# One-hot rows on ScalarE for every batch, neighbour rows gathered in groups of four tiles, and a new order of work in a four-layer graph network

## The chip, the core and the metric

The kernel runs on one core of one Trainium2 chip. Five engines take part, each with its own queue of instructions that it works off in order: TensorE (PE in the profile, with its weight loads as PEld), VectorE (DVE), ScalarE (ACT), GpSimd (POOL) and SyncE (SP), which here only issues DMAs. ScalarE and GpSimd issue DMAs too. The metric is the device time in microseconds of one execution, as the median over several executions.

## What is computed

Input are 32 graphs ("batches") of 512 nodes with 128 features each, `x`, and a 0/1 adjacency matrix per graph, `adj`, in which about 3% of the entries are 1. Four layers follow each other, each with a layer norm and a ReLU ahead of it and a residual sum behind it. The first is a maximum over neighbours, the others are products with the adjacency matrix and with weights:

```python
# layer 0: edge maximum
p = einsum('bnd,do->bno', h, W1 - W2)
q = einsum('bnd,do->bno', h, W2)
x = x + max over j of relu(p[:, :, None, :] + q[:, None, :, :] + b) * adj[..., None]
# layer 1: four rounds, with features of earlier rounds appended
src_agg = einsum('bjv,bij->biv', src, l2norm(adj, 2))
dst_agg = einsum('bjv,bji->biv', dst, l2norm(adj, 1))
f = tanh(concat([src_agg, self_rep, dst_agg]) @ wu + bu)
# layer 2: mean over neighbours, then a weight
x = x + einsum('bnm,bmf->bnf', adj / rowsum, h @ weight) + bias
# layer 3: four GRU rounds
m = einsum('bjn,bjd->bnd', adj, hidden @ weight[i])
hidden = gru_cell(m, hidden, ...)
```

## The kernel before, in words

A batch's 512 nodes are four tiles (`NT = 4`) of 128 partitions. The kernel has no loop on the chip: all 32 batches are written out in one stream. Each batch goes through `prepare` (layer norm, transposed adjacency `at`, the products `qn` and `pn`, counts and keys of neighbours), `gathers` (the edge maximum), `layer1` and `layer23`.

The edge maximum needs, for every node, the largest row of `qn` among its neighbours. It is taken in two ways whose results are merged.

- By one-hot rows. For each of the four source tiles `jt` and each slot `k` of 1 to 4 (`KSLOT`), a 128x1024 one-hot matrix `oh` is made from counts `ccd`; two matmuls with the parts `qhl` pick the rows into a PSUM bank `pa`, and VectorE keeps the running maximum in `acc`. VectorE makes `oh` with one comparison (L1139), or ScalarE makes it with two activations, `far` and then `oh` (L1136 and L1137). How many of the four slots go to ScalarE is set by `ONACT` (L34), read by `min(b, len(ONACT) - 1)`: two for batches 0 and 1, one for batch 2, none from batch 3 on.
- By DMA. What lies beyond the slots is fetched row by row from a table `qtab` in device memory, by indices `idx`, seven rounds (`NLEFT`) for each of the four tiles, so 28 indirect DMAs a batch from GpSimd's queue. Round 0 lands in `gm`; every later row lands in a buffer `G` of one tile, of which there are four, and VectorE takes the maximum of `gm` and `G` for that tile (L1127).

`gm` and `acc` are merged in the stage "first". `parts` splits a feature matrix into `hi` (ScalarE) and `lo` (VectorE), or `sbuf_parts` makes `lo` on GpSimd; `aggregate` multiplies both with the adjacency into the bank `pg`. `pu` is the sum of a round of layer 1, `pk`, `phn` and `pxn` are the gates of layer 3. `gate`, `zc`, `nn`, `h` are the tensors of the GRU cell.

The order of instructions is not the order of the code. `Flow` records each operation with a cost and with what it depends on, and `step` then picks operations one by one as a planner: among those that could start first on an engine, the one with the earliest due time. A due time is `n * pace - due - lead` (L451): the place of the batch times `PACE`, less the planned work behind the operation, less a lead of its stage. Leads are in `LEADS`, with additions for the first and last batch in `LEADS0` and `LEADSN`; `FIRST`, `LAST` and `WEIGHTS` shift the places of the first batches, the last batches and the weight preparation. `SPACING` keeps the gathers' due times apart (`spaced`). Six parts are open at a time (`AHEAD`). Operations marked `port` are planned one at a time, since GpSimd and VectorE are taken to share an access to SBUF (L298). Where the planner sees TensorE idle for over a microsecond, it puts in filler matmuls, `spin` (L553), [...]whose result is not used.

All operations recorded this way carry line L529 in the profile, so the groups are read by the names of their tiles.

Of the kernel before, what the change touches and what calls it, by code (L numbers as in the profile page):

```python
# [13 lines left out]
F32 = mybir.dt.float32  # L14
# [10 lines left out]
P = 128  # L25
# [5 lines left out]
ROWS = 1024  # L31
KEY = float(ROWS)
CODES = ((0, 1), (P, 1), (2 * P, 2), (4 * P, 4))
ONACT = (2, 2, 1, 0)  # L34
NLEFT = 7
PACE = 46.14
SPACING = 1.5
AHEAD = 6
BANKS = (1, 2, 2, 1)

LEADS = {
    "prepare": -28.3, "counts": -7.5, "keys": 16.5, "rows": 26.6,
    "gather0": 59.4, "gather1": 70.0, "gather2": 28.0, "gather3": 53.5,
    "first": 61.2, "layer1": 43.0, "layer10": 30.3, "layer11": 8.7,
    "layer12": 56.0, "layer13": -41.3, "layer2": 39.7, "layer3": 5.5,
    "layer30": 99.5, "layer31": 189.8, "layer32": 213.5, "layer33": 84.7,
    "out": 56.0,
}

LEADS0 = {  # L50
    "prepare": 18.5, "counts": 53.1, "keys": 4.8, "rows": -15.7,
    "gather0": 52.2, "gather1": 93.4, "gather2": -34.5, "gather3": -69.1,
    "first": 0.5, "layer1": 141.7, "layer10": 10.1, "layer11": 110.3,
    "layer12": -73.8, "layer13": -13.4, "layer2": 6.9, "layer3": 56.5,
    "layer30": 35.3, "layer31": 29.8, "layer32": 117.9, "layer33": 64.0,
    "out": 75.9,
}
LEADSN = {
    "prepare": -19.9, "counts": -18.3, "keys": -42.0, "rows": 46.6,
    "gather0": 15.9, "gather1": -47.7, "gather2": -77.8, "gather3": -4.3,  # L60
    "first": 13.3, "layer1": -33.7, "layer10": 14.0, "layer11": -36.5,
    "layer12": 103.7, "layer13": 62.6, "layer2": 212.2, "layer3": 99.8,
    "layer30": 182.6, "layer31": 105.8, "layer32": 85.0, "layer33": 161.6,
    "out": -15.2,
}
FIRST = (1.57, 0.36, -0.05, 0.0)
LAST = (0.0, 0.18, 0.33, 0.24, 0.3)
WEIGHTS = (-3.98, -2.44, -5.94)

LATE = {  # L70
    "xn2": ("xn0", 1), "hi2": ("qn", 1), "lo2": ("gm", 1), "mT": ("acc", 1), "hg": ("hT0", 1),
# [114 lines left out]
def in_sbuf(v):  # L186
    return not isinstance(v, View) or v.tile.sbuf
# [86 lines left out]
class Engine:  # L274
# [5 lines left out]
    def __getattr__(self, op):  # L280
        fn = getattr(self.real, op)

        def note(*args, **kw):
            outs, ins = [], []
            for i, v in enumerate(args):
                (outs if i == 0 else ins).append(v)
            for k, v in kw.items():
                (outs if k in ("out", "accum_out") else ins).append(v)
            ins = [v.ap if isinstance(v, Rows) else v for v in ins]
            outs, ins = ([v for v in vs if hasattr(v, "free_size")] for vs in (outs, ins))  # L290
            cost, after = self.flow.cost(self.name, op, outs, ins)
            self.flow.note(self.name, fn, args, kw, outs, ins, cost, after)


            tensors = [v for v in ins if v.free_size() >= 64 and in_sbuf(v)]
            fast = self.name == "vec" and op == "tensor_scalar"
            if self.name == "vec" or (self.name == "pool" and op.startswith("tensor")):
                self.flow.part[-1].port = fast or len(tensors) > 1  # L298

        return note  # L300


class Flow:
# [46 lines left out]
    def fixed(self, t, shape, dtype):  # L350

        return View(Buf(None, 0, shape[0], t), shape, dtype)
# [270 lines left out]
class FastWeights:  # L623
# [5 lines left out]
    def __init__(self, nc, F, a, const, mid, ps):  # L629
        self.F, self.mid, self.ps = F, mid, ps  # L630
        self.NL3 = a["L3_gnn_weight"].shape[0]
        n = a["x"].shape[1]

        def fixed(shape, dtype, name):
            return const.tile(shape, dtype, name=name)

        ident = fixed([P, P], F32, "ident")
        make_identity(nc, ident)
        identb = fixed([P, P], BF16, "identb")
        nc.vector.tensor_copy(identb, ident)  # L640
        self.ident, self.identb = ident, identb
        self.mhalf = fixed([P, 8], F32, "mhalf")
        nc.gpsimd.memset(self.mhalf, -0.5)

        self.ones = fixed([P, P], F32, "ones")
        nc.gpsimd.memset(self.ones, 1.0)
        ltf = fixed([P, P], F32, "ltf")  # L650
        nc.gpsimd.affine_select(
            ltf, self.ones, pattern=[[1, P]], compare_op=ALU.is_ge, fill=0.0, base=0,
            channel_multiplier=-1,
        )
        nc.gpsimd.memset(ltf[0:HP, HP:P], 0.0)
        self.lt = fixed([P, P], F32R, "lt")
        nc.vector.scalar_tensor_tensor(self.lt, ident, NBASE, ltf, ALU.mult, ALU.add)
        self.ltk = fixed([P, P], BF16, "ltk")
        nc.vector.tensor_scalar(self.ltk, self.lt.bitcast(F32), KEY, None, ALU.mult)
        self.code = fixed([P, n // P, P], BF16, "code")  # L660
        icode, code = fixed([P, n // P], I32, "icode"), fixed([P, n // P], F32, "fcode")
        for t, (first, step) in enumerate(CODES):
            nc.gpsimd.iota(
                icode[:, t : t + 1], pattern=[[1, 1]], base=first, channel_multiplier=step
            )
        nc.vector.tensor_copy(code, icode)
        for t in range(n // P):
            nc.vector.tensor_scalar(
                self.code[:, t, :], ident, code[:, t : t + 1], None, ALU.mult
            )  # L670


        self.sign = fixed([P, 2], F32, "sign")
        nc.gpsimd.memset(self.sign[:, 0:1], -1.0)
        nc.gpsimd.memset(self.sign[:, 1:2], 1.0)
        nc.gpsimd.memset(self.sign[0:4, 0:1], 1.0)
        nc.gpsimd.memset(self.sign[0:4, 1:2], 0.0)

        self.slot = fixed([P, KSLOT + 1], F32, "slot")
        for k in range(KSLOT + 1):  # L680
            nc.gpsimd.memset(self.slot[:, k : k + 1], -(NBASE + k))
        self.nc, self.a, self.const, self.n = nc, a, const, n
        self.rows = self.zeros([P, n // P, P], "rows")
        self.vectors = []
        for i in range(2):
            t = fixed([P, P], F32, f"vectors{i}")
            nc.gpsimd.memset(t, 0.0)
            self.vectors.append(F.fixed(t, [P, P], F32))

    def own(self, shape, dtype, name):  # L690
        return self.F.tile(self.const, shape, dtype, name, name)
# [167 lines left out]
def fast(ctx: ExitStack, tc: tile.TileContext, a: dict, out: bass.AP, bad):  # L859
    nc = tc.nc  # L860
# [3 lines left out]
    NT = N // P  # L864

    const = ctx.enter_context(tc.tile_pool(name="const", bufs=1))
# [3 lines left out]

    F = Flow(nc, PACE, AHEAD)
    F.share(ps, 8, {f"ps{s}": n for s, n in enumerate(BANKS)} | {"idle": 0})
# [11 lines left out]
    big = ctx.enter_context(tc.tile_pool(name="big", bufs=1))  # L884
    mid = ctx.enter_context(tc.tile_pool(name="mid", bufs=1))
    W = FastWeights(nc, F, a, const, mid, ps)

    zero = const.tile([P, P], F32, name="zero")  # L890
    nc.gpsimd.memset(zero, 0.0)
    tables, scals = [], []
    for i in range(2):
        t = dram.tile([ROWS, P], F32, name=f"qtab{i}")
        k = (ROWS - 2 * P) // P
        nc.sync.dma_start(
            out=t[2 * P :, :].rearrange("(k p) d -> p k d", p=P),
            in_=zero.unsqueeze(1).to_broadcast([P, k, P]),
        )
        tables.append(F.fixed(t, [ROWS, P], F32))  # L900
        scals.append(F.fixed(dram.tile([6, N], F32, name=f"scal{i}"), [6, N], F32))
# [211 lines left out]
    def gathers(b, at, ccd, qhl, pn, tab, idx, has, dinv):  # L1113
        acc = F.tile(mid, [P, N], F32, tag="acc", name=f"acc_{b}")
        gm = F.tile(mid, [P, NT, P], F32, tag="gm", name=f"gm_{b}")
        for r in range(NLEFT):
            for it in range(NT):


                G = gm[:, it, :]  # L1120
                if r:
                    G = F.tile(big, [P, P], F32, tag="G", name=f"G_{b}_{it}_{r}", bufs=4)
                F.pool.indirect_dma_start(
                    out=G, out_offset=None, in_=tab, in_offset=Rows(idx[:, it, r : r + 1])
                )
                if r:
                    F.vec.tensor_max(gm[:, it, :], gm[:, it, :], G)  # L1127
                    F.spaced("gather", SPACING if b else 1.3)
        for jt in range(NT):
            F.lead = lead(b, f"gather{jt}")  # L1130
            for k in range(1, KSLOT + 1):
                oh = F.tile(big, [P, 2, N], F32R, tag="oh", name=f"oh_{b}_{jt}_{k}", bufs=3)
                if k > KSLOT - ONACT[min(b, len(ONACT) - 1)]:

# [224 lines left out]
    def spin(n):  # L1359
# [5 lines left out]
    places = [  # L1365
        b - FIRST[min(b, len(FIRST) - 1)] - LAST[max(0, b - B + len(LAST) - 1)] for b in range(B)
    ]
    F.run(
        list(zip(WEIGHTS, (W.first, W.rest, W.last)))
        + [(p, partial(batch, b)) for b, p in enumerate(places)]  # L1370
# [471 lines left out]
```

## Time and profile before

| what | us |
|---|---|
| median of three executions | 2909.99 (2907.28 to 2910.49) |
| the profiled execution | 2910.69 |
| its span, first to last instruction | 2909.0 |

The granted TensorE clock was 0.993 of full speed on average. Some groups that the text comes back to:

| group | engine | count | mean ns | busy us |
|---|---|---|---|---|
| oh<-ccd, 128x1024 | VectorE | 492 | 723 | 348.9 |
| gm<-gm,G, 128x128 | VectorE | 768 | 322 | 242.4 |
| acc<-acc,pa, 128x512 | VectorE | 992 | 679 | 673.4 |
| far<-ccd, 128x1024 | ScalarE | 20 | 1150 | 23.0 |
| oh<-far, 128x1024 | ScalarE | 20 | 1150 | 23.0 |
| G<-qtab, one tile's rows | GpSimd | 768 | 1095 | 841.3 |
| gate<-h,gate, 128x512 | GpSimd | 132 | 1326 | 175.1 |
| spin | TensorE | 233 | 400 | 64.1 |

A group is a set of instructions with the same tiles. "Out<-in" names the tile that is written and those that are read. Busy times of one engine can overlap at the edges of two instructions. Idle time of an engine is given with the instruction that ended it ("<- DVE lo" is a wait for VectorE's writing of `lo`). The chain of waits follows the last instruction back, at each step to what released it.

### The profile page before, as it was taken

The page shows a single profiled execution, that of the slowest core. Times are in us where ns is not written, and L with a number is a line of the kernel's source. Part 1 is how long each engine was busy: PE and PEld are TensorE (multiplying, and loading weights), DVE is VectorE, ACT ScalarE, POOL GpSimd, SP SyncE. Part 2 cuts the span into 40 slices and gives each one's busy share as a digit, 9 for nine tenths or more (in the row PEclk, how much of TensorE's full clock was granted, in tenths as well). Part 3 has the DMA queues.
Part 4 walks back from the last instruction along what each step waited for, and adds up shares of the span by engine and source line. Part 5 has one row for each costly group of instructions (what it writes and reads, how often), then busy time and mean ns, then how long its engine had stood idle before and what let it go on. Part 6 is the DMA issues. An engine that isn't in the chain of part 4 may idle for free.

```text
span 2909.0 us, 38588 instructions
## 1 busy us (share of the span) xinstructions
PE 2795.8 (96%) x11766; PEld 1794.6 (62%) x11766; DVE 2299.1 (79%) x5371; ACT 1268.4 (44%) x2622; POOL 1848.5 (64%) x2020
## 2 busy tenths in 40 slices
PE   7799999999999999999999999999999999999998
PEld 4565566666666665666665666666666666566675
DVE  6778888788888888888788888888888888887634
ACT  6643344444444443444443444444444444443333
POOL 3666656666666766666766666776666666666522
PEclk9999999999999999999999999999999999999999
DMA  6644334323444433334423344433344433333200
GB/s 150 136 74 88 62 85 81 83 55 76 79 86 81 83 60 78 74 83 80 87 56 78 74 84 87 82 69 64 74 84 87 81 81 56 70 66 63 55 5 9
DMA packets 191270, 218.49 MB, mean 75 GB/s; under 512 B 30376, under 2 KB 139600, under 8 KB 191056
## 3 DMA queue, kind: packets, MB, share of 16 engines
q0 software_dynamic: 47104, 92.34, 23.1%
q1 hardware_dynamic: 73768, 63.63, 7.1%
q10 hardware_dynamic: 70184, 59.98, 6.8%
q8 instruction: 96, 1.57, 0.2%
q14 instruction: 118, 0.97, 0.1%
HBM read 164.32 MB, written 17.96 MB: 63 GB/s over the span
## 4 chain that ended last, share of the span: by engine, by line
PE 85%; DVE 7%; DMA 2%; issue 2%; ACT 2%; POOL 1%; SPq 0%; ACTq 0%; DVEq 0%; POOLq 0%
PE pg L529 26%; PE pu L529 19%; PE pk L529 14%; PE pa L529 7%; PE phn L529 4%; PE pxn L529 4%; DVE acc L529 3%; PE ph L529 2%; PE pq L529 2%; PE pkey L529 2%; PE pt L529 1%; DVE lo L529 1%; PE pf L529 1%; PE po L529 1%; PE px L529 1%
## 5 line engine op out<-in xcount | busy, mean ns | idle before, releaser
L529 POOL DMA_INDIRECT G<-qtab,idx x768 | 841.3, 1095 | 653.6 <-DVE gm L529 495.3
L529 DVE TENSOR_TENSOR acc<-acc,pa 128x512 f32<-128x512 f32 x992 | 673.4, 679 | 123.3 <-PE pa L529 97.6
L529 PE MATMUL pg<-an,lo 128*128 128x512 f32 (+1 forms) x1072 | 461.9, 433 | 0.0
L529 PE MATMUL pg<-an,hi 128*128 128x512 f32 (+1 forms) x1072 | 456.1, 428 | 4.8 <-PE spin L553 1.1
L529 PE MATMUL pa<-oh,qhl 128*128 128x512 f32 x1024 | 450.5, 508 | 6.1 <-DVE acc L529 2.1
L529 PE MATMUL pu<-ag,w 128*128 128x512 f32 (+1 forms) x952 | 448.0, 568 | 4.1 <-DVE ag L529 4.1
L529 DVE TENSOR_SCALAR oh<-ccd 128x1024 fp32r<-128x1024 bf16 x492 | 348.9, 723 | 62.4 <-PE pa L529 55.0
L529 ACT ACTIVATE xn<-x,shift,rstd 128x128 f32<-128x128 f32 x512 | 214.6, 483 | 261.4 <-POOL shift L529 255.7
L529 PE MATMUL pg<-at,lo 128*128 128x512 f32 (+1 forms) x672 | 295.9, 442 | 22.8 <-DVE lo L529 22.3
L529 PE MATMUL pg<-at,hi 128*128 128x512 f32 (+1 forms) x672 | 272.7, 407 | 8.4 <-ACT hi L529 7.2
L529 PEld LDWEIGHTS pa<-oh,qhl 128*128 128x128 f32 x1024 | 191.8, 193 | 135.5 <-issue 65.9
L529 PEld LDWEIGHTS pg<-an,hi 128*128 128x128 f32 x1072 | 202.6, 189 | 107.2 <-issue 62.5
L529 PEld LDWEIGHTS pg<-an,lo 128*128 128x128 f32 x1072 | 202.7, 189 | 85.9 <-issue 52.0
L529 PE MATMUL pk<-h,g_hh 128*128 128x512 f32 (+1 forms) x528 | 246.7, 582 | 1.2 <-DVE ag L529 1.1
L529 DVE TENSOR_TENSOR gm<-gm,G 128x128 f32<-128x128 f32 x768 | 242.4, 322 | 3.5 <-DMA G<-qtab,idx 3.3
L529 PE MATMUL pk<-mT,g_ih 128*128 128x512 f32 (+1 forms) x528 | 243.3, 580 | 0.5 <-ACT mT L529 0.5
L529 PEld LDWEIGHTS pu<-ag,w 128*128 128x128 f32 x952 | 177.0, 189 | 107.7 <-issue 80.3
L529 ACT ACTIVATE gate<-pk,bsum 128x512 f32<-128x512 f32 (+1 forms) x264 | 176.7, 672 | 151.3 <-PE pk L529 148.7
L529 DVE TENSOR_TENSOR ag<-pg,rbc 128x512 f32<-128x512 f32 (+1 forms) x272 | 172.5, 653 | 71.5 <-PE pg L529 69.7
L529 DVE SCALAR_TENSOR_TENSOR nn<-phn,bcol,gate 128x512 f32<-128x512 f32 (+1 forms) x132 | 96.3, 729 | 148.2 <-ACT gate L529 148.1
L529 ACT COPY mT<-pg 128x512 f32<-128x512 f32 (+1 forms) x164 | 94.3, 575 | 272.9 <-PE pg L529 265.4
L529 POOL TENSOR_TENSOR rstd<-rstd,mhalf 128x4 f32<-128x4 f32 x128 | 152.7, 1193 | 86.9 <-DVE shift L529 82.6
(178 smaller groups left out, 5146.7 us busy)
## 6 DMA issues: line engine op xcount, KB each, us to landing
af<-in_adj_dram ACTq DMA_DIRECT2D x32, 1024.0 KB
ccd<-cc SPq DMA_DIRECT2D x512, 64.0 KB
an<-in_adj_dram POOLq DMA_DIRECT2D x128, 256.0 KB, 3.4
x<-in_x_dram ACTq DMA_DIRECT2D x64, 256.0 KB
rbc<-scal SPq DMA_DIRECT2D x32, 512.0 KB
G<-qtab,idx POOLq DMA_INDIRECT x768, 3.9
qtab<-qn SPq DMA_DIRECT2D x128, 64.0 KB
out_dram<-xo ACTq DMA_DIRECT2D x32, 256.0 KB
```

The costliest lines, as they stand in the source:

```text
L529: op.fn(*(real(v) for v in op.args), **{k: real(v) for k, v in op.kw.items()})
```

## The change

There are three parts. One of the four slots goes to ScalarE in every batch from 3 on. The rows of one round are gathered for all four tiles into one buffer `G` of four tiles, of which there are two (`GROUPS`), and one maximum of 128x512 takes them into `gm`. To make room in SBUF, the tiles `zero` and two `vectors` are replaced by one new tile `blank` and by `ltf`, which is cleared once it has been read. All parameters of the order are set anew, and the planner marks some more GpSimd operations as `port`.

```diff
-ONACT = (2, 2, 1, 0)
+ONACT = (2, 2, 1, 1)
 NLEFT = 7
-PACE = 46.14
-SPACING = 1.5
+GROUPS = 2
+PACE = 45.43
+SPACING = 9.6
...
 LEADS = {
-    "prepare": -28.3, "counts": -7.5, "keys": 16.5, "rows": 26.6,
-    "gather0": 59.4, "gather1": 70.0, "gather2": 28.0, "gather3": 53.5,
+    "prepare": -75.2, "counts": -7.0, "keys": -14.1, "rows": 10.4,
+    "gather0": 64.0, "gather1": 12.2, "gather2": 2.3, "gather3": 19.7,
...
-FIRST = (1.57, 0.36, -0.05, 0.0)
-LAST = (0.0, 0.18, 0.33, 0.24, 0.3)
-WEIGHTS = (-3.98, -2.44, -5.94)
+FIRST = (2.19, 1.09, -0.22, 0.0)
+LAST = (0.0, 0.0, -0.44, 0.72, -1.27)
+WEIGHTS = (-3.99, -3.16, -6.01)
...
-                self.flow.part[-1].port = fast or len(tensors) > 1
+                two = self.name == "pool" and sum(in_sbuf(v) for v in ins) > 1
+                self.flow.part[-1].port = fast or two or len(tensors) > 1
...
+        self.blank = fixed([P, P], F32, "blank")
+        nc.gpsimd.memset(self.blank, 0.0)
...
-        self.vectors = []
-        for i in range(2):
-            t = fixed([P, P], F32, f"vectors{i}")
-            nc.gpsimd.memset(t, 0.0)
-            self.vectors.append(F.fixed(t, [P, P], F32))
+        nc.gpsimd.memset(ltf, 0.0)
+        self.vectors = [F.fixed(t, [P, P], F32) for t in (ltf, self.blank)]
...
-    zero = const.tile([P, P], F32, name="zero")
-    nc.gpsimd.memset(zero, 0.0)
...
-            in_=zero.unsqueeze(1).to_broadcast([P, k, P]),
+            in_=W.blank.unsqueeze(1).to_broadcast([P, k, P]),
...
         for r in range(NLEFT):
+            G = F.tile(big, [P, NT, P], F32, tag="G", name=f"G_{b}_{r}", bufs=GROUPS) if r else gm
             for it in range(NT):
-                G = gm[:, it, :]
-                if r:
-                    G = F.tile(big, [P, P], F32, tag="G", name=f"G_{b}_{it}_{r}", bufs=4)
                 F.pool.indirect_dma_start(
-                    out=G, out_offset=None, in_=tab, in_offset=Rows(idx[:, it, r : r + 1])
+                    out=G[:, it, :], out_offset=None, in_=tab, in_offset=Rows(idx[:, it, r : r + 1])
                 )
-                if r:
-                    F.vec.tensor_max(gm[:, it, :], gm[:, it, :], G)
-                    F.spaced("gather", SPACING if b else 1.3)
+            if r:
+                F.vec.tensor_max(gm, gm, G)
+                F.spaced("gather", SPACING if b else 4.0)
```

The other leads, and those of the first and last batch, change in the same way.

## The prediction

> **What bounds the kernel now.** I read the page's busy line first, then the waits of TensorE in the steady part of the run, then its timeline around those waits, and last the groups that the change touches.
>
> ```profile
> PE 2795.8 (96%) x11766; PEld 1794.6 (62%) x11766; DVE 2299.1 (79%) x5371; ACT 1268.4 (44%) x2622; POOL 1848.5 (64%) x2020
> ...
> PE 85%; DVE 7%; DMA 2%; issue 2%; ACT 2%; POOL 1%; SPq 0%; ACTq 0%; DVEq 0%; POOLq 0%
> ```
>
> TensorE is busy 96% of the span and makes 85% of the chain of waits; the change takes no matmul away. Whatever it brings has to come from time in which TensorE does not work. That is 2909.0 - 2795.8 = 113.2 us of idle time, and 64.1 us of filler matmuls (the group "spin", 233 of them, whose result nothing reads), which count as busy: 177 us in all. By stretches (busy time of stages; idle plus spin): 0 to 180 us 40.1 + 32.5 = 72.6; 180 to 450 us 12.3 + 5.5 = 17.8; 450 to 2520 us 41.9 + 18.6 = 60.5; the end 19.1 + 7.5 = 26.6. Between 450 and 2520 the long pieces of the chain return every 86.4 us (1301.83, 1388.25, ...): that is one batch, and the stretch holds 24 of them, so 2.5 us are lost per batch. The waits of TensorE in that stretch say where:
>
> ```profile
> PE pg L529 <- DVE lo L529: 21.1, 24, 0.9
> PE spin L553 <- DVE lo L529: 8.3, 23, 0.4
> PE pg L529 <- ACT hi L529: 5.5, 24, 0.2
> ```
>
> Columns: total us, times, longest. Twenty-four times each, so two fixed places in every batch, and both wait for VectorE's "lo". The timeline of one batch shows the first:
>
> ```profile
> 1333.24 1.31 POOL L529 TENSOR_TENSOR gate<-h,gate 128x512 f32<-128x512 f32 x1
> ...
> 1333.38 1.33 DVE L529 TENSOR_TENSOR gm<-gm,G 128x128 f32<-128x128 f32 x1
> ...
> 1334.22 0.58 ACT L529 CAST hi<-pf 128x512 fp32r<-128x512 f32 x1 [0.37 <-PE pf L529]
> ...
> 1334.63 1.47 DVE L529 TENSOR_TENSOR acc<-acc,pa 128x512 f32<-128x512 f32 x2
> ...
> 1336.02 0.68 DVE L529 TENSOR_TENSOR lo<-pf,hi 128x512 fp32r<-128x512 f32 x1
> ...
> 1336.76 0.50 PE L529 MATMUL pg<-at,lo 128*128 128x512 f32 x1 [0.89 <-DVE lo L529]
> ```
>
> The reader should see a small row maximum that takes 1.33 us beside a POOL operation, two acc maxima pushed back behind it, lo behind those, and TensorE behind lo. hi was there at 1334.80; lo could have been ready at 1335.48 and was ready at 1336.70: 1.2 us late. The second place is at 1379: lo ends at 1378.99, three spins follow, and pg starts only at 1380.00. This costs 0.36 of wait and nearly 1 us of filler that turned out unnecessary.
>
> **What the Trainium skill says.** (1) "SBUF — State Buffer", section "Who interferes with whom": a VectorE instruction with two SBUF inputs contends with a GpSimd instruction that reads SBUF, and the second to issue blocks. The trace agrees: gm<-gm,G has a median of 281 ns, a mean of 322 and a maximum of 1576, and the slow one above ran beside gate<-h,gate. (2) "VectorE: DVE Perf Modes", section on the TRN2 errata: the SBUF cost is a fixed part per instruction, so larger tiles pay it less often. The trace agrees only partly: 281 ns for 128 columns, 666 for 512 (h<-gate,nn), so four small ones cost 1124 against 666 by their records; but consecutive starts in the timeline lie 0.20 and 0.60 us apart, so the engine's own time is 0.80 against 0.60. (3) "Perfetto Trace Analysis", section "Optimizing Scalar/DVE Operations": work that both engines can do may be moved to ScalarE where VectorE is saturated. VectorE here is at 71.6 of 86.4 us per batch, ScalarE at 37.7: near saturation, not at it.
>
> **The change, part by part.**
> One-hot rows. ONACT's last entry counts for every batch from 3 on: 29 batches x 4 source tiles = 116 VectorE comparisons (oh<-ccd, mean 723 ns, 0.60 from start to start) go away, and 116 far and 116 oh activations come to ScalarE (1150 ns each in the rows of the first three batches). Per batch: VectorE -4 x 0.60 = -2.4 us, ScalarE +8 x 1.15 = +9.2 us, from 37.7 to about 47 of 86.4. ScalarE's own waits for TensorE are far larger (mT alone 272.9 us in the run), so its capacity covers this; what is not covered is its order. It runs in order, and behind each 1.15 us activation stand hi, mT, gate and f, for which TensorE waits.
>
> Row maxima. 24 maxima over 128 columns per batch become 6 over 512: 24 x 0.20 = 4.8 us against 6 x 0.60 = 3.6, so -1.2. Collisions: now (322 - 281) x 24 = 1.0 us per batch; a two-input operation of 512 (nn<-nn,zc) has mean 850 against 686 for gm<-gm,px, which has one input in PSUM: 0.16 x 6 = 1.0. Equal in sum, but at 6 places in place of 24. VectorE comes to about 71.6 - 3.6 = 68 us per batch.
>
> Gathers. The same 28 DMAs (1095 ns each on POOL). POOL waits 495.3 us in the run for gm maxima, because a tile's buffer comes back only after its maximum. With two buffers of four tiles a group takes some 4 x 1.4 us of issue (0.3 lies between two), 3.9 to land and 0.7 for the maximum, about 10 us, and two overlap: 6 groups need 30 to 60 us of the 86.4. Below: those POOL waits vanish. Above: one late maximum holds four issues, and what stands behind them on POOL (lo, gate, zc, rstd, and the 4 loads of an) comes up to 10 us later. POOL is off the chain (1%), so I take nothing and keep up to 1 us per batch for the range.
>
> Setup. One memset fewer and one that must wait until lt has been read (VectorE, 0.64 us at 2.60). Other engines are still waiting for loads then (wsq until 9.18), so it costs nothing; without that cover below 1 us. The table's zeroing DMA has another source only.
>
> Order. All leads, PACE, FIRST, LAST and WEIGHTS differ, so every instruction of five queues may stand elsewhere: SP's copies of ccd (512) and qtab, ACT's loads of af and x, POOL's of an. SP waits 707.6 us for pn and 615.2 for px, so it has room. The order also decides what the freed VectorE time becomes. Nothing in the trace prices it. Lower bound of the time: all 60.5 us of the steady part and some 12 at the edges go, 2910 - 72 = 2838. Upper bound: new stalls as large as the present ones in every batch, 2910 + 27 x 2.5 = 2978.
>
> Sum of the likeliest case. At the first place the 1.2 us of lateness mostly goes, since the colliding maximum is a quarter as frequent and fewer comparisons stand in the way; I take the stall from 0.89 + 0.23 = 1.12 to 0.3: -0.82. At the second, half of 1.32 us (gap from 1378.68 to 1380.00) goes, as the filler is planned from a gap that a freer VectorE makes shorter: -0.66. That is 1.48 us per batch. Late next is then hi, on ScalarE. It holds from 180 us to about 2520: 27 batches x 1.48 = 40 us. Edges: ONACT is unchanged for batches 0 to 2 and the start waits for loads (w 4.0, graw 4.6 us), so nothing, +-20. The profiled execution lasted 2910.7 us (span 2909.0), the median of three is 2910.0: the difference is below what is taken here. 2910 - 40 = 2870.
>
> **The rivals.**
> A, forecast: TensorE's gaps shrink, 2870 (2838 to 2900). For it: both steady gaps end with a VectorE instruction. Against it: the gaps are 2.9% of a batch at most, so the gain is small at best.
> B, the stalls belong to an order and not to a load: one gap closes, another of the same size opens; 2910. For it: VectorE has 15 us of idle time per batch already and the gaps are there nevertheless.
> C, slower: ScalarE's queue. Each batch gets eight 1.15 us activations ahead of hi, mT, gate and f, and a hit at one of these delays TensorE by up to 1.15 us. It decides against the change from 1.48 / 1.15 = 1.3 full hits per batch. At 2.3: 27 x (2.3 x 1.15 - 1.48) = 31 us, so 2941. For it: TensorE already waits 24 times for hi, and batches carry about 20 such ScalarE instructions. Against it: ScalarE idles more than half of a batch, and the waits for hi are 0.2 us.
> D, the groups do not shorten anything because gathers are hidden: true already in A's sum, where they count nothing; it gives A without 0.4 to 0.8 us per batch, 2881 to 2892, and lies in A's range.
>
> **How the numbers follow.** A with D 0.57, B 0.08, C 0.35. A measurement of this kernel tells about 0.2%, or 6 us, from no change, so faster means below 2904. Range: 2838 leaves 0.05 below; up to 2945 takes in B and more than half of C and leaves about 0.14. A's own range is 2838 to 2900.
>
> **What would show it.** Right: the line "pg <- lo" of TensorE's steady waits falls from 0.9 us per batch to below 0.4, the spins per batch from 3 to 0 or 1, the chain repeats every 84.9 us or so, VectorE shows 376 oh and 192 gm<-gm,G of 128x512, ScalarE 136 far. Wrong by C: TensorE waits for hi, mT or gate with far or oh just ahead of them on ScalarE. Wrong by POOL: lo<-xn or gate<-h late behind four DMA issues. Wrong in size: the period is unchanged and the difference sits in the first 180 or last 390 us, which the new order moves and I could not price.

## The result, and the profile after

| kernel | median us | ratio to the kernel before, 95% interval | span of the profiled execution |
|---|---|---|---|
| before | 2907.2 (2905.5 to 2910.49) | 1 | 2909.0 |
| changed | 2921.73 (2919.94 to 2923.92) | 1.0049 (1.0039 to 1.006) | 2919.7 |

The changed kernel is slower by half a per cent, about 14 us, where 40 us were forecast to be gained. The granted clock is 0.992 against 0.993 on average; it is lower only in the first 180 us (0.90 against 0.93) and the same in both kernels from there on (0.99, then 1.00). TensorE's matmuls of those 180 us that are no spins take 165 ns in the mean in both kernels, so the clock is not the reason.

The first lines are the busy line and the chain of the page of the changed kernel.

```profile
PE 2794.7 (96%) x11731; PEld 1786.7 (61%) x11731; DVE 2196.1 (75%) x4679; ACT 1509.8 (52%) x2854; POOL 1831.3 (63%) x2019
...
PE 75%; DVE 7%; POOL 7%; issue 4%; DMA 4%; ACT 3%; SPq 0%; DVEq 0%; POOLq 0%; ACTq 0%
```

VectorE lost 103 us of work and ScalarE gained 241, as intended. TensorE's busy time did not move, 2794.7 against 2795.8, though the run is longer. What moved is the chain: GpSimd's share in it rose from 1% to 7%, and TensorE's fell from 85% to 75%.

The waits of TensorE in the same stretch as before, 450 to 2520 us (total us, times, longest):

```profile
PE pg L531 <- POOL lo L531: 24.8, 21, 1.2
PE ph L531 <- DVE h L531: 14.9, 20, 0.7
PE pu L531 <- ACT mT L531: 3.8, 6, 2.0
```

The lines "pg <- DVE lo", "spin <- DVE lo" and "pg <- ACT hi" of the kernel before are gone, and of its 69 spins in this stretch 8 are left. Two others stand in their place, again some 20 times each, so again two fixed places in every batch: up to 1.2 us for `lo` of GpSimd, up to 0.7 us for `h`. The timeline shows where they come from. First `lo`:

```profile
1661.01 1.28 POOL L531 DMA_INDIRECT G<-qtab,idx  x1 [0.15 <-issue]
...
1662.57 0.62 ACT L531 CAST hi<-xn 128x512 fp32r<-128x512 f32 x1
1662.59 1.00 POOL L531 DMA_INDIRECT G<-qtab,idx  x1 [0.30 <-issue]
...
1663.90 0.94 POOL L531 DMA_INDIRECT G<-qtab,idx  x1 [0.30 <-issue]
...
1664.87 1.27 POOL L531 TENSOR_TENSOR lo<-xn,hi 128x512 fp32r<-128x512 f32 x1
...
1666.19 0.50 PE L531 MATMUL pg<-at,lo 128*128 128x512 f32 x1 [1.19 <-POOL lo L531]
```

`lo` needs `hi`, which is there at 1663.19. But GpSimd works its queue off in order, and three gathers stand ahead of `lo`; the last of them is through at 1664.84. `lo` is 1.7 us late and TensorE waits 1.19 us of that. Then `h`:

```profile
1590.57 1.13 POOL L531 DMA_INDIRECT G<-qtab,idx  x1 [0.30 <-issue]
...
1591.39 2.16 DVE L531 TENSOR_TENSOR h<-gate,nn 128x512 f32<-128x512 f32 x1
...
1591.71 1.28 POOL L531 TENSOR_TENSOR x<-x,b 128x512 f32<-128x512 f32 x1
...
1593.61 0.65 PE L531 MATMUL ph<-ident,h 128*128 128x128 f32 x4 [0.74 <-DVE h L531]
```

`h` lasts 2.16 us, where its median in the kernel before is 0.68. It has two inputs in SBUF, and it ends 0.56 us after `x<-x,b` of GpSimd has ended, as if it had done its work only then. TensorE transposes `h` next and waits 0.74 us.

The batches end as follows (start of the first `xo` of a batch in VectorE's timeline, us; batches are counted from 0):

| end of batch | 1 | 2 | 3 | 4 | 5 |
|---|---|---|---|---|---|
| before | 367.5 | 474.7 | 561.1 | 648.3 | 734.8 |
| changed | 381.4 | 474.5 | 567.8 | 659.9 | 746.2 |

From batch 4 on both take 86.4 us in most batches (before 2034.01 to 2120.40, changed 2043.07 to 2129.38). The difference is 11 to 12 us up to batch 9; then single batches of either kernel are a microsecond or two longer: it lies between 7.5 and 10 us in batches 11 to 26, and the spans differ by 10.7 us. So there are two questions: why the steady batch gained nothing, and where the 11 us at the start went. The table seems to put them into batches 3 and 4; the windows say that they were lost earlier. Busy time of the engines (PE, PEld, DVE, ACT, POOL, with the number of instructions), clock, DMA share and GB/s, first of the kernel before, then of the changed one:

```profile
180.00:450.00 270.00, 257.75 (x1050) 161.11 (x1049) 220.66 (x509) 116.78 (x241) 174.23 (x189) 0.99 0.36 71
```

```profile
180.00:450.00 270.00, 253.58 (x1035) 154.97 (x1034) 206.90 (x430) 135.32 (x258) 174.20 (x186) 0.99 0.42 73
```

The 1035 matmuls of the changed kernel contain 43 spins, those of the kernel before 21. Idle time and spins together are 16.4 + 10.7 = 27.1 us, against 12.3 + 5.5 = 17.8: 9.3 us lost between 180 and 450. Batch 2 nevertheless ends at the same time in both, because the changed kernel has by then done less of the batches that follow: up to 475 us it has issued 1892 matmul instructions less 160 spins, 1732, and the other 1918 less 136, 1782. Batches 3 and 4 pay for it.

### The profile page after: what moved, and what is told of

The parts are those of the page before. It is cut to its first block, busy times and chain, and to the rows that moved or that the text cites. A ratio compares the mean times of both kernels' runs of the same rounds, so it can differ in the third digit from the quotient of the medians.

```text
span 2919.7 us, 37742 instructions
## 1 busy us (share of the span) xinstructions
PE 2794.7 (96%) x11731; PEld 1786.7 (61%) x11731; DVE 2196.1 (75%) x4679; ACT 1509.8 (52%) x2854; POOL 1831.3 (63%) x2019
## 4 chain that ended last, share of the span: by engine, by line
PE 75%; DVE 7%; POOL 7%; issue 4%; DMA 4%; ACT 3%; SPq 0%; DVEq 0%; POOLq 0%; ACTq 0%
PE pg L531 23%; PE pu L531 16%; PE pk L531 14%; PE pa L531 6%; PE phn L531 4%; PE pxn L531 3%; POOL G L531 3%; DMA out_dram<-xo 2%; DVE h L531 2%; PE ph L531 2%; PE pkey L531 2%; DVE ag L531 1%; PE pf L531 1%; DVE acc L531 1%; POOL lo L531 1%
## 5 line engine op out<-in xcount | busy, mean ns | idle before, releaser
L531 POOL DMA_INDIRECT G<-qtab,idx x768 | 821.0, 1069 | 335.6 <-issue 171.0
L531 PE MATMUL pa<-oh,qhl 128*128 128x512 f32 x1024 | 433.1, 502 | 9.3 <-DVE oh L531 5.2
L531 PE MATMUL pg<-at,lo 128*128 128x512 f32 (+1 forms) x672 | 308.6, 461 | 26.9 <-POOL lo L531 26.8
L531 POOL TENSOR_TENSOR rstd<-rstd,mhalf 128x4 f32<-128x4 f32 x128 | 143.8, 1123 | 270.0 <-DVE shift L531 269.2
L531 DVE TENSOR_SCALAR oh<-ccd 128x1024 fp32r<-128x1024 bf16 x376 | 267.4, 726 | 15.0 <-DMA ccd<-cc 12.4
L531 POOL TENSOR_SCALAR zc<-gate 128x512 f32<-128x512 f32 x132 | 98.1, 743 | 241.6 <-ACT gate L531 240.7
```

The costliest lines, as they stand in the source:

```text
L531: op.fn(*(real(v) for v in op.args), **{k: real(v) for k, v in op.kw.items()})
```

## Experiments

**Parts alone, planned anew.** The first four kernels each take one part of the change (`e2_oldorder` two of the three), and the planner orders everything with the parameters of one kernel or the other. The kernel before in this batch: 2909.05.

`e1_order`, the code of before with the new parameters of the order:

```diff
-PACE = 46.14
-SPACING = 1.5
+PACE = 45.43
+SPACING = 2.4
...
-                self.flow.part[-1].port = fast or len(tensors) > 1
+                two = self.name == "pool" and sum(in_sbuf(v) for v in ins) > 1
+                self.flow.part[-1].port = fast or two or len(tensors) > 1
...
-                    F.spaced("gather", SPACING if b else 1.3)
+                    F.spaced("gather", SPACING if b else 1.0)
```

All leads, `FIRST`, `LAST` and `WEIGHTS` are those of the changed kernel too.

> Code of the kernel before (ONACT 2,2,1,0, one tile's rows in G) with the new leads, PACE, FIRST, LAST, WEIGHTS and the new port rule; the gathers' spacing is a fourth of the new one. Theory S (the four-tile groups hold GpSimd and cost the 11 us of the first 450 us, and the steady 86.4 us per batch don't depend on the order): within 6 us of before, 2902 to 2914. Theory O (the new order itself is what costs, wherever it is applied): 2917 to 2930. Theory A (ScalarE's new activations cost): as S.

`e2_oldorder`, the changed code with the order parameters of before (`SPACING` times four, as the groups have four tiles):

```diff
-PACE = 45.43
-SPACING = 9.6
+PACE = 46.14
+SPACING = 6.0
...
-                F.spaced("gather", SPACING if b else 4.0)
+                F.spaced("gather", SPACING if b else 5.2)
```

> Code of the changed kernel (ONACT 2,2,1,1, groups of four) with the old leads, PACE, FIRST, LAST, WEIGHTS and the old port rule; spacing four times the old one. Theory S: 2917 or more, with the loss in the first 450 us. Theory O: 2901 to 2913. Theory A: 2917 or more, with the loss spread over all batches.

`e3_onact`, the code and order parameters of before, with ScalarE's share alone:

```diff
-ONACT = (2, 2, 1, 0)
+ONACT = (2, 2, 1, 1)
```

> Kernel before with ONACT (2,2,1,1) alone. Theory S: 2902 to 2914, since nothing is gained in the steady part and groups are absent. Theory O: the same. Theory A: 2917 or more, over all batches. If VectorE's load set the steady gaps, as was forecast, about 2870 to 2890.

`e4_groups`, the kernel before with the groups of gathers and the new tiles alone, `SPACING` 6.0 (5.2 for batch 0):

> Kernel before with the groups of four tiles alone (and the SBUF room made for them), old order, spacing four times the old one. Theory S: 2917 or more, lost before 450 us. Theory O and theory A: 2902 to 2914.

Measured: order 3137.07, ratio 1.0788 (1.077 to 1.0806); old order under the new code 3006.28, 1.0332 (1.0315 to 1.035); ScalarE's share 2960.25, 1.0177 (1.016 to 1.0194); groups 3018.8, 1.038 (1.0362 to 1.0397). Each is slower than the whole change, by 38 to 215 us, and no reading fits all four: `e1_order` lies outside all of them, and the "2917 or more" that S and A give for some of the others is met without the rest of what they say. The waits of TensorE in `e1_order` show why the times say nothing of the parts (450 to 2520 us):

```profile
PE spin L554 <- DVE acc L530: 14.6, 16, 3.2
PE ph L530 <- DVE h L530: 12.4, 15, 1.7
PE pt L530 <- ACT xn L530: 11.5, 10, 2.7
```

These are other places, hit in some batches and not in others. The leads fit one set of operations and durations; with another set the planner deals all five queues anew. The times of these four runs are inconclusive on the parts.

Their traces tell one thing, though. GpSimd's gathers and what ended its idle time before them, in the kernel before, in `e1_order` (new order parameters, no groups), in `e4_groups` (old order parameters, groups) and in the changed kernel:

```profile
L529 POOL DMA_INDIRECT G<-qtab,idx x768 | 841.3, 1095 | 653.6 <-DVE gm L529 495.3 <-DVE st L529 52.0 <-issue 49.6
L530 POOL DMA_INDIRECT G<-qtab,idx x768 | 823.9, 1073 | 819.5 <-DVE gm L530 591.6 <-issue 59.0 <-DVE idx L530 37.3
L530 POOL DMA_INDIRECT G<-qtab,idx x768 | 822.4, 1071 | 289.9 <-issue 184.4 <-DVE gm L530 51.8 <-DMA ccd<-cc 10.4
L531 POOL DMA_INDIRECT G<-qtab,idx x768 | 821.0, 1069 | 335.6 <-issue 171.0 <-DVE gm L531 81.8 <-DVE shift L531 55.0
```

The waits for `gm` go and the gathers run one straight behind the other ("issue") where the groups are there, under either set of order parameters. The groups alone don't put `lo` late: TensorE waits for GpSimd's `lo` 6 times in this stretch of `e4_groups` (5.7 us) and once in `e2_oldorder` (0.3 us), against 21 times in the changed kernel. For that, the place of `lo` behind three gathers, batch after batch, is needed too, and this place comes with the order of the whole change.

**Single operations moved.** In all further kernels the planned order of one of the two kernels stands in the code as data, spins included, and the operations are issued in that order. So everything is issued in the order it had, but for what an edit moves. (All lines then have one number, L1031 or the like.) Two readings were set against each other. C: both kernels lose in two fixed places per batch, the places differ, and each can be taken away by itself; that both take 86.4 us is chance. R: 86.4 us has one common reason, and what is won in one place is lost in another.

`r1_lo` and `r2_lo_x2`, the changed kernel. In 23 batches the `lo` that was late goes ahead of the last two of the three gathers in front of it; in `r2_lo_x2` also the sum `x<-x,b` (the tile `x2`) goes behind the gather that follows it, where one does, so that it meets `h` no more:

```diff
+        q = queue()
+        for i, op in enumerate(q):
+            if re.fullmatch(r"lo_\d+_1", name(op)) and gather(q[i - 1]) and gather(q[i - 2]):
+                behind(q[i - 1], op)
+                behind(q[i - 2], op)
+        q = queue()
+        for i, op in enumerate(q):
+            if name(op).startswith("x2_") and gather(q[i + 1]):
+                behind(op, q[i + 1])
```

(`queue` lists GpSimd's operations in order, and `behind(a, b)` puts `a` behind `b`. The first loop alone is `r1_lo`.)

> The changed kernel's order replayed with the first kind of move alone: lo<-xn of layer 1 ahead of the two gathers in front of it; the bias addition x<-x,b stays. If the two waits cost what they show, 1.2 us per batch goes and 0.7 stays: 24 batches by 1.2 to 1.4, 2888 to 2895. If the second wait grows as the first goes (VectorE's h meets x<-x,b later and longer): 2900 to 2918.

> The changed kernel with its order written down and replayed, and two kinds of moves on GpSimd alone: in layer 1 the split lo<-xn goes ahead of the two gathers in front of it, and the bias addition x<-x,b goes behind the gather that follows it. Theory C (the two steady gaps of the changed kernel, 1.2 us for GpSimd's lo behind gathers and 0.7 us for VectorE's h held by x<-x,b, are what its order lost on the chip): both waits go, a batch takes 84.4 to 85.2 us, 2870 to 2893. Theory R (86.4 us per batch is set by something that both kernels share, such as a loop through layer 3's single buffers, and gaps only fill up with it): 2914 to 2926 with other waits of the same sum. If the moves disturb more than they mend: above 2926.

| kernel | median us | ratio, 95% interval | batch us | end of batch 4 |
|---|---|---|---|---|
| changed | 2921.73 | 1.0049 (1.0039 to 1.006) | 86.4 | 659.9 |
| `r1_lo` | 2891.84 | 0.9951 (0.9934 to 0.9968) | 84.9 | 656.9 |
| `r2_lo_x2` | 2867.07 | 0.9861 (0.9844 to 0.9877) | 84.05 | 661.3 |

The first move is worth 1.5 us per batch, the second 0.85, and both together 55 us; the batch is somewhat shorter than C expected (84.4 to 85.2). Each move brings more than TensorE's recorded wait (1.0 and 0.6 us per batch in the mean), and no run shows where the rest was. TensorE's waits in `r2_lo_x2` (450 to 2520 us) show that nothing came in their place:

```profile
PE pu L1031 <- ACT mT L1031: 4.6, 11, 2.1
PE pg L1031 <- ACT hi L1031: 1.6, 1, 1.6
PE px L1031 <- ACT f L1031: 1.5, 1, 1.5
PE ph L1031 <- DVE h L1031: 0.5, 1, 0.5
```

"pg <- POOL lo" fell from 24.8 us to nothing and "ph <- DVE h" from 14.9 to 0.5. That GpSimd's `x` had held `h` is seen in VectorE's group of `h`, of the changed kernel and then of `r2_lo_x2` (busy us, mean ns):

```profile
L531 DVE TENSOR_TENSOR h<-gate,nn 128x512 f32<-128x512 f32 x132 | 120.9, 917 | 5.7 <-POOL gate L531 1.5 <-DVE nn L531 0.5
```

```profile
L1031 DVE TENSOR_TENSOR h<-gate,nn 128x512 f32<-128x512 f32 x132 | 91.1, 691 | 5.8 <-POOL gate L1031 1.5 <-DVE nn L1031 0.5
```

`r5_bfix` and `r7_bspin`, the kernel before. In `r7_bspin` the spins of batches 5 to 26 are left out, 63 in all. In `r5_bfix` also the row maximum that ran beside `gate<-h,gate` goes behind `lo`:

```diff
+        for n, part in enumerate(made):
+            for op in part if 8 <= n < 30 else ():
+                self.spins.pop(id(op), None)
...
+        q = [op for op in order if op.engine == "vec"]
+        for i, op in enumerate(q):
+            if re.fullmatch(r"lo_\d+_1_1", name(op)) and 5 <= int(name(op).split("_")[1]) < 28:
+                behind(q[i - 3], op)
```

> The kernel before with its order replayed, without the three filler matmuls per batch of batches 5 to 26, and with one row maximum (the one that took 1.33 us beside gate<-h,gate) moved behind lo in batches 5 to 27. Theory C (as the prediction said of the kernel before: the colliding maximum and the needless filler are its steady gaps): 22 batches shorter by 0.9 to 1.2 and by about 0.9 us, a batch of 84.3 to 84.8, 2862 to 2872. Theory R: 2903 to 2912, a batch of 86.4. If the fillers kept the clock up: a lower granted clock and more than 2912.

> The kernel before with its order replayed and only the three fillers per batch of batches 5 to 26 left out. If they were needless, as the prediction read them: 22 x 0.9 = 20 us less, 2884 to 2892, a batch of 85.4 to 85.6. If something else held pg there: 2903 to 2912.

Without the spins: 2888.56, ratio 0.9945 (0.9928 to 0.9961), 85.5 us per batch. With the maximum moved too: 2863.6, ratio 0.9849 (0.9833 to 0.9865), 84.5 us per batch. The granted clock of the profiled executions is 0.993 and 0.994, so it did not need these spins. TensorE's waits for VectorE's `lo`, first of `r7_bspin`, then of `r5_bfix` (450 to 2520 us):

```profile
PE pg L1040 <- DVE lo L1040: 28.8, 45, 0.9
```

```profile
PE pg L1040 <- DVE lo L1040: 9.8, 23, 1.1
PE pg L1040 <- ACT hi L1040: 5.5, 24, 0.2
```

Without spins both places show as waits of `pg`; moving the maximum takes the first one away, and 0.4 us per batch stay at the second.

C holds in both kernels, and R falls: each loses some 2 us per batch in two places of its own, and most of this can be had back without a new loss. `r5_bfix` is the fastest kernel of this study, 43.6 us below the kernel before; `r2_lo_x2` stands 3.5 us above it, and their intervals overlap. So some 40 us can be gained over the kernel before, with the change and without it.

**Is the change's own work felt?** Reading V says that the relief of VectorE is what the batch time rests on. `r3_noact` is the changed kernel with `ONACT = (2, 2, 1, 0)`: the share that the change had moved to ScalarE in batches 3 and later goes back to VectorE, at the places where ScalarE's second activation stood. `r6_lo_x2_noact` does that on `r2_lo_x2`. `r4_max4` makes four maxima of 128x128 out of each one of 128x512:

```diff
-                F.vec.tensor_max(gm, gm, G)
+                for it in range(NT):
+                    F.vec.tensor_max(gm[:, it, :], gm[:, it, :], G[:, it, :])
```

> The changed kernel's order replayed, with the one-hot rows that went to ScalarE for batches 3 to 31 made on VectorE again, each at the place of ScalarE's second activation. Theory V (VectorE's freed time is what the new order needs, 2.4 us per batch): 2950 to 2990. Theory N (VectorE's load doesn't matter in the steady part, the gaps sit elsewhere): 2915 to 2930. Theory A (ScalarE's activations cost time): below 2915.

> The changed kernel's order replayed, with four maxima of 128x128 in place of one of 128x512, at the same place; buffers and gathers as in the changed kernel. Theory V: 1.2 us of VectorE per batch more and more meetings with GpSimd, 2935 to 2960. Theory N: 2917 to 2928. In both the first 450 us stay as in the changed kernel.

> Both moves on GpSimd, and in addition the one-hot rows of batches 3 to 31 back on VectorE at the same places. Theory N2 (ScalarE's share isn't needed in the steady part even when the gaps are gone): a batch within 0.3 us of 84.05, loss only in the first five batches, 2873 to 2885. Theory V2 (VectorE becomes the next bound once the gaps are gone): a batch of 85.5 to 86.5, 2900 to 2930.

| kernel | median us | ratio, 95% interval | batch us | end of batch 4 |
|---|---|---|---|---|
| `r3_noact` | 2933.16 | 1.0088 (1.0072 to 1.0105) | 86.5 | 671.8 |
| `r4_max4` | 2929.59 | 1.0076 (1.0059 to 1.0093) | 86.6 | 666.0 |
| `r6_lo_x2_noact` | 2875.8 | 0.9896 (0.988 to 0.9913) | 84.0 | 664.6 |

The work that the change takes off VectorE is worth nothing in the steady part: with it or without, a batch takes the same time to 0.2 us. `r3_noact` and `r4_max4` come out 2 to 3 us above what N expects and below V; `r6_lo_x2_noact` is what N2 expects. So V falls there. By the ends of batch 4 the relief is worth 3 to 12 us once, at the start, and the large maximum 6. VectorE's old stalls do not come back either: in this stretch TensorE waits for VectorE's `lo` once in `r3_noact` (0.8 us) and in `r6_lo_x2_noact` (0.4 us), and not at all in `r4_max4`. So it is not the smaller load of VectorE, part by part, that keeps them away. The new order and the groups are left, and no run tells these two apart (nor are both parts of the relief taken back at once).

**The 11 us at the start.** `r8_start` is `r2_lo_x2` without the spins of batches 2 to 8 (34 fewer in all):

> Both moves on GpSimd, and without the fillers of batches 2 to 8 (30 matmuls, about 8 us of busy time between 180 and 540 us). If part of the start's loss is needless filler: 2 to 8 us below the run with both moves, 2859 to 2865. If the fillers stand in real gaps: the same, 2864 to 2872. If the clock falls without them: more.

2869.69, ratio 0.9876 (0.986 to 0.9893), the same as `r2_lo_x2` within the noise: the spins stand in gaps that are there anyway. The next kernels test GpSimd's queue. An operation of GpSimd that is no gather goes ahead of up to two gathers that stand straight in front of it:

```diff
+        last = max(i for i, op in enumerate(order) if name(op).startswith("xo_3"))
+        early = {id(op) for op in order[:last]}
+        for op in queue():
+            if id(op) not in early or gather(op) or op.fn.__name__ == "dma_start":
+                continue
+            for _ in range(2):
+                q = queue()
+                i = q.index(op)
+                if i and gather(q[i - 1]) and ...:
+                    behind(q[i - 1], op)
```

`r9_early` has this and the moves of `r2_lo_x2`, `r10_early` this alone:

> Kernel of r2 (steady lo ahead of two gathers, x's sum behind the next one), and for every GpSimd operation planned before the end of batch 2 that is no gather: it goes ahead of up to two gathers that stand straight in front of it. Theory G, the gathers hold GpSimd in the start as they do in the steady part: the 11 us lost by the end of batch 4 fall to 0 to 7, so that batch 4 ends at 649 to 656 us in place of about 660, and the time is 4 to 11 us below r2's 2867: 2856 to 2863. Theory O, the order of the first batches itself (what stands behind what on TensorE, VectorE and ScalarE): batch 4 ends at 658 to 662, the time is 2864 to 2872. A result above 2875 would say that the early gathers, held back by the moves, are needed where they stood.

> Changed kernel with the early moves of GpSimd's operations alone, steady part left as it is. Theory G: 4 to 11 us below the changed kernel's 2921.7, so 2911 to 2918, with the batch period still 86.4. Theory O: 2919 to 2925. If r9 gains and this one doesn't, the gain depends on what the steady part can hold.

Measured: 3004.12, ratio 1.0324 (1.0309 to 1.0338), and 3032.88, ratio 1.0426 (1.0412 to 1.0441). The condition "xo_3" is also met by `xo_30` and `xo_31`, so the moves reach every batch and not the first ones alone, and the numbers are to be read so: GpSimd's other work ahead of the gathers everywhere costs 111 to 137 us. `r11_early2` and `r12_early2` compare with `== "xo_3"` and end there:

> As r9, with the early moves really ended at batch 3's output (some 26 places). Theory G, gathers hold GpSimd in the start: batch 4 ends at 649 to 656 us in place of about 660, time 2856 to 2863. Theory O, the order of the first batches itself: batch 4 ends at 658 to 662, 2864 to 2872. Third reading, T, from r9, in which batch 4 ended 25 us later (685.9): the row gathers are themselves late in the start, and putting anything ahead of them costs; then batch 4 ends at 670 to 690 and the time is 2880 to 2900.

> As r10, with the early moves ended at batch 3's output, on the changed kernel with its steady part as it is. Theory G: 2911 to 2918; O: 2919 to 2925; T: 2930 to 2950. In all three the batch period from batch 5 on stays 86.4.

Measured: 2891.72, ratio 0.994 (0.9922 to 0.9958), batch 4 ends at 678.5; and 2946.84, ratio 1.0128 (1.011 to 1.0147), batch 4 ends at 681.9, and the two batches after that one take 86.3 and 86.6. Both are what the third reading, T, expects: putting GpSimd's other work one or two gathers earlier in the first four batches costs 25 us. The traces show how: in the first 570 us of `r11_early2` the `rstd` that went ahead waits for its own input 13 times, where it did so 6 times in `r2_lo_x2`, and holds the gathers behind it; the 140th gather (28 make a batch) starts at 431.5 us in place of 410.2. The opposite is done by `r13_gfirst` and `r14_gfirst_rstd`: on `r2_lo_x2`, up to batch 3, a gather goes ahead of the operation in front of it.

```diff
+            if id(op) not in early or gather(op) or op.fn.__name__ == "dma_start" or not re.match("rstd_|shift_|gate|zc", name(op)):
+                continue
+            q = queue()
+            i = q.index(op)
+            if gather(q[i + 1]) and ...:
+                behind(op, q[i + 1])
```

(`r13_gfirst`; in `r14_gfirst_rstd` the pattern is `rstd_|shift_` alone.)

> Kernel of r2; up to batch 3, a gather that stands straight behind one of GpSimd's rstd, shift, gate or zc goes ahead of it, some 12 places. Theory T, the gathers come late in the start: 3 to 10 us below r2's 2867, so 2857 to 2864, and batch 4 ends below 658. Theory L, GpSimd's order is at its best locally and the 9.4 us come from other engines: 2866 to 2880, batch 4 ends at 660 to 672.

> As r13, with rstd and shift alone passed, some 8 places, so that TensorE's gate and zc keep theirs. Theory T: 2858 to 2866. Theory L: 2866 to 2874.

Measured: 2876.94, ratio 0.9884 (0.9868 to 0.9901), batch 4 ends at 668.9; and 2877.4, ratio 0.9893 (0.9876 to 0.9909), at 660.2. No gain either, the second a little above what L expects. None of these moves of GpSimd's operations betters the start, in either direction, so the 9.3 us lost there probably come from elsewhere. TensorE's timeline of 180 to 300 us in the changed kernel shows single waits for VectorE, ScalarE and GpSimd, two of which are:

```profile
192.36 1.02 PE L555 MATMUL spin<-code,identb 128*128 128x512 bf16 x4 [1.95 <-DVE acc L531]
...
207.02 0.49 PE L531 MATMUL pg<-at,hi 128*128 128x512 f32 x1 [1.81 <-ACT hi L531]
```

Which of the new order's many moves brought them stays open; no run isolates it.

## Why the prediction was wrong

- **The bound, and the two places: right.** The stalls behind VectorE's `lo` were real and could be had back. `r7_bspin` puts the needless spins at 0.9 us per batch ("nearly 1 us"), and `r5_bfix` both places at 1.9 of the 2.5 us that are lost.
- **That the change closes them: the outcome right, the reason not.** "pg <- lo" of VectorE fell from 0.9 us per batch to nothing, and the spins in that stretch from 69 to 8. I took 1.48 us. `r2_lo_x2`, the changed kernel without its new stalls, takes 84.05 us, so the gain ahead of these is 86.4 - 84.05 = 2.35. But the forecast had it from a freer VectorE ("the colliding maximum is a quarter as frequent and fewer comparisons stand in the way"). With the comparisons back on VectorE a batch takes 84.0 us (`r6_lo_x2_noact`), and neither these nor four small maxima (`r4_max4`) bring the stalls behind VectorE's `lo` back. That they went was luck as far as this reason goes.
- **"Late next is then hi, on ScalarE": this step failed.** TensorE's wait for `hi`, 5.5 us before, is not among the waits of that stretch any more. Late next were GpSimd's `lo` and VectorE's `h`, 1.5 and 0.85 us per batch by `r1_lo` and `r2_lo_x2`: together the 2.35 us that had been gained, so that the batch came back to 86.4.
- **"POOL is off the chain (1%), so I take nothing and keep up to 1 us per batch": the term that was mis-sized.** It measured 1.5 us per batch for the queue (`r1_lo`). The share of the chain was that of a kernel in which a gather waited for its buffer (495.3 us for `gm` maxima). With groups this wait is 81.8 us, gathers run back to back, and in the new order `lo` stands behind three of them. The planner counts 1.05 us for a gather (`cost`), where gathers that follow each other start 1.25 us apart or more. By this the plan is 2.4 us or more too early for the 12 gathers that stand in the 18.5 us ahead of the `lo` shown, which was 1.7 us late. Whether the planner put `lo` there for this reason is not shown, as no run changes this cost. The prediction named this sign ("lo<-xn or gate<-h late behind four DMA issues") and the bound ("comes up to 10 us later"), and then priced it by the share of GpSimd in the old chain.
- **Collisions "equal in sum, but at 6 places in place of 24": wrong in place, 0.85 us per batch (`r2_lo_x2` against `r1_lo`).** The large maximum was to last 850 ns and has a mean of 708, so it hardly collides. The collision went to `h`, whose mean rose from 666 to 917 ns: 0.25 x 132 / 32 = 1.0 us per batch. Its partner was GpSimd's `x<-x,b`, which the sum did not have. `r4_max4` shows that the size of the maximum is not what matters there: 86.6 us per batch with small ones. (The 666 ns read for a maximum of 512 columns is the mean of `h` with eight half-size ones in it; those of 512 columns last 682. It changes nothing in the sum.)
- **Loads of the engines: right, and without effect.** VectorE 1638.13 / 2070 x 86.4 = 68.4 us per batch (68 forecast), ScalarE 1098.95 / 2070 x 86.4 = 45.9 (47). `r6_lo_x2_noact` shows that the steady part doesn't need this relief.
- **Rivals.** C, ScalarE's queue, falls by `r3_noact` and `r6_lo_x2_noact`. B, one gap closes and another of the same size opens, is what the steady part did, and it had been given 0.08: stalls that belong to an order and not to a load. Its 2910 lacks the start. D, hidden gathers that shorten nothing, is not tested by itself.
- **Edges "nothing, +-20": +11 measured**, inside that bound, of which 9.3 us are lost between 180 and 450 us; their cause stays open. They make the kernel slower and not merely equal, since the steady part came out near zero.

The step that failed is the price of the gathers, taken at nothing, together with "late next is then hi": I asked whether GpSimd was on the chain, and not what would be on it once its waits for buffers had gone. Its queue took back 1.5 us per batch, and its `x<-x,b` beside `h` another 0.85, which is the whole gain.

## What to carry to other kernels

Where a change takes away waits of an engine that is off the chain, operations of its queue move together: look at what stands behind those that now run back to back, and at which operations of VectorE and GpSimd now meet. Price this from the queue itself (three gathers ahead of `lo` at about 1.3 us each, where the planner counts 1.05), not from the engine's share in the chain of the kernel before. Before a new order is sought for a kernel that loses 2 us per batch in two fixed places, move the two operations: that gave 44 us in this one kernel with one operation per batch moved and the spins of batches 5 to 26 left out, and no other part of the kernel touched.

## What the runs showed of the hardware

- Indirect DMAs back to back on GpSimd start 1.25 to 1.6 us apart in nine of ten cases, though each is mostly recorded with 0.94 to 1.3 us; a gap of 0.30 us named "issue" lies between them. In the groups shown above this gap adds up to 171.0 us in the changed kernel, where the kernel before has 49.6.

  The Trainium skill, "Perfetto Trace Analysis", section "GPSIMD Engine Instruction", says that a GpSimd instruction's recorded span is not to be relied on and that the spacing of starts is to be taken; the numbers here agree.
- The shared port: the Trainium skill, "SBUF — State Buffer", section "Who interferes with whom", says that whichever issues first holds it. `h` is recorded from 1591.39, 0.32 us ahead of GpSimd's `x`, and ends 0.56 us after it. So the recorded start doesn't tell which had the port. That `x` was the partner is shown by `r2_lo_x2`, which moves it. The price was 1.5 us for `h` (2.16 against 0.68) and 0.23 us in the mean of all 132.
- In the first four batches, GpSimd's other operations put ahead of one or two gathers cost 25 us (`r11_early2` against `r2_lo_x2`), and gathers put ahead of one of them gained nothing (`r13_gfirst`, `r14_gfirst_rstd`).
- 63 filler matmuls fewer in the steady part left the granted clock at 0.993 (`r7_bspin`) and gave 0.9 us per batch.
